# A graph-attention, scan and feed-forward kernel: the passes of its two layers alternate, the comparisons that rank its keys are spread over three passes, and its preparations are cut into smaller steps

## The chip, the core and the metric

The kernel runs on one core of a Trainium2 chip. The metric is the device time of one execution in microseconds (us). A core has five engines that run at once and wait for each other: PE (matmuls; weight loads are shown apart as PEld), DVE (vector work), ACT (activations and copies), POOL (more vector work) and SP, which here only issues DMAs. PE writes into PSUM, which has few tiles to go round; the other engines empty them.

## What is computed

The input is 16 rows of 32 channels by 512 numbers, and coordinates of 512 points for each row. Three parts follow each other, each added to the running result:

```python
x = x + xattn(ctx_4096, layernorm(x), ...)   # graph part, two layers
x = x + attn(layernorm(x), ...)              # scan part: projections, a short convolution, a masked product
x = x + ffn(layernorm(x), ...)               # feed-forward with a low-rank term
```

The graph part sorts the 512 points of every row in four ways (two Morton keys, two Hilbert keys). A point's neighbours are the ten points round it in such an order. For every point, the differences to its neighbours go through a small attention of ten by ten, a linear map and a convolution; an instance norm over the row, a leaky ReLU and the greatest over the ten neighbours give the layer's output. Layer 2 does the same with layer 1's output as its features, and a last small convolution joins the input and both layers.

```python
g1 = graph_features(f0, inds, perm1, W1, b1); h1 = lrelu(inorm(conv1(g1))); feats1 = h1.max(-1)
g2 = graph_features(feats1, inds, perm2, W2, b2); h2 = lrelu(inorm(conv2(g2))); feats2 = h2.max(-1)
out = lrelu(inorm(conv3(concat(feats, feats1, feats2))))
```

## The kernel before, in words

The change touches the graph part alone. It treats the 16 rows as four groups `g` of four rows, 128 partitions each, and makes eight **passes**, one for each group and layer. `order` (line 984) lists them: groups 0 and 1 in layer 1, then 0 and 1 in layer 2, then 2 and 3 in layer 1, then 2 and 3 in layer 2. In the code `layer` is 0 for the first layer and 1 for the second; the text calls their passes **first-layer** and **second-layer** passes, and counts passes 0 to 7. The first layer has 32 output channels, the second 64, so a matmul of `mapped` (line 874) has 128 columns in the one and 256 in the other.

A pass has 43 **blocks** (`gi`, 12 points each), and the loop of line 1019 goes through all 344 blocks as a software pipeline: one turn works on several blocks, each at another step (the number is how many blocks the step lags behind).

- `scores` (0): a mask matmul (line 805, the first matmul of a block) and 16 score matmuls (line 812) into PSUM tile `s`. `greatest` (0): DVE takes the greatest of each row (line 821). `expo` (1): PE subtracts it (line 829), ACT takes the exponential (line 834). `sums` (1) and `shares` (1): DVE sums (841) and inverts (847), POOL multiplies into `EN` (849). `turn` (3): DVE transposes it (855).
- `mapped` (0): 48 matmuls of the differences `DD` with the weights (874), which ACT copies out of PSUM (879). `outputs` (3): 32 matmuls into `h` (902). `reduce` (4) and `rest` (5): DVE takes greatest and moments out of `h` (919 to 928).
- `differences` runs six blocks ahead (`LEAD`) on POOL (line 770), out of the sorted features `fs` and the centres `crep`; SP then copies them into `DX` by DMA (line 780).

Three other kinds of work are cut into small steps (Python generators) and put between those, and every engine takes its instructions in the order in which they are issued:

- **Comparisons** (`compare`, line 535): the rank of a point is found by comparing all keys with all: a matmul of 512 columns (538) into one of two PSUM tiles `misc`, and a Sign on ACT that sums its row (539). There are 256 of them, 16 for each row. `rank_step` does one. 64 are done before the blocks begin; then each block does one (line 1033), and a second one while fewer than 128 are done (line 1042).
- **The preparation** of the next pass (`prep`, line 621): for the first layer the layernorm that gives its features `U` (lines 88 to 93); four transposes on PE (`pf`, line 634) and a copy on ACT; a split into three bf16 parts on DVE (641, 643); two casts `c16`, `c32` (647, 650) and a matmul `ph` (655). Then, for each of four rows and four chunks of points, four **one-hots** on DVE (line 723, from the ranks) and 12 matmuls with them (`place`, 689) that sort the features. The sorted row leaves PSUM by an ACT copy `so` (696), goes out to DRAM (`store`, 700), and comes back spread over partitions as `fs` (`spread`, 709); `tick` counts the steps between those. The last instruction, a DVE copy that widens `fs` (line 741), needs the last `spread` to have landed. `steps` (line 998) gives a preparation one or two of its steps a block: two while more steps are left (of a guess, `PREP` = 45) than blocks. What is left is issued all at once at block 37 (line 1047), where `differences` begins to need the next pass's `fs`.
- **The tail** of a pass (`end`, line 944): instance norm, leaky ReLU, and for the second layer the last convolution and its layernorm (`finish`, 970). A tail begins at block 3 of the next pass and takes the steps of `steps` for itself until it is done; the preparation waits for it.

The two steps that the prediction speaks of most are these (lines 646 to 657; a step ends at a `yield`):

```python
        c32 = wk.tile([P, D], F32, tag="c32", name=f"c32{key}", bufs=1)
        nc.vector.tensor_copy(c32, c16)
        yield
        hc = wk.tile([P, npair, D], F32, tag="hc", name=f"hc{key}")
        for pr in range(npair):
            ph = ps_1.tile([P, D], F32, tag="misc", bufs=2, name=f"ph{key}_{pr}")
            nc.tensor.matmul(ph, lhsT=WC[:, pr], rhs=c32, start=True, stop=True)
```

The scan and the feed-forward parts follow (from line 1055 on) and are the same in both kernels.

Of the kernel before, what the change touches and what calls it, by code (L numbers as in the profile page):

```python
# [18 lines left out]
P = 128  # L19
# [26 lines left out]
NHT = 16  # L46
LR = 18
LEAD = 6
PREP = 45


@with_exitstack
def kernel(ctx: ExitStack, tc: tile.TileContext, I, out):
# [31 lines left out]
    def layernorm_steps(pool, dst, src, key):  # L85

        st = pool.tile([P, 6], F32, tag="ln_st", name=f"lnst_{key}")
        nc.vector.bn_stats(st, src)
        mv = pool.tile([P, 2], F32, tag="ln_mv", name=f"lnmv_{key}")
        nc.vector.bn_aggr(mv, st)  # L90
        r = pool.tile([P, 1], F32, tag="ln_r", name=f"lnr_{key}")
        yield from rstd_steps(pool, r, mv[:, 1:2], 1, key)
        nc.vector.tensor_scalar(dst, src, mv[:, 0:1], r, ALU.subtract, ALU.mult)
# [282 lines left out]
def graph_part(nc, tc, cx, I, dram, id32, ones, xt, F0, layernorm_steps, rstd_steps, scan_input):  # L376
# [241 lines left out]
    def later_tile(n):  # L618
        return ps_1.tile([P, D], F32, tag="misc", bufs=2, name=f"kd{n}")

    def prep(g, layer, early=False):


# [22 lines left out]
        c16 = wk.tile([P, D], F16, tag="c16", name=f"c16{key}", bufs=1)  # L646
        nc.vector.tensor_copy(c16, src)
        yield
        c32 = wk.tile([P, D], F32, tag="c32", name=f"c32{key}", bufs=1)
        nc.vector.tensor_copy(c32, c16)  # L650
        yield
        hc = wk.tile([P, npair, D], F32, tag="hc", name=f"hc{key}")
        for pr in range(npair):
            ph = ps_1.tile([P, D], F32, tag="misc", bufs=2, name=f"ph{key}_{pr}")
            nc.tensor.matmul(ph, lhsT=WC[:, pr], rhs=c32, start=True, stop=True)
            nc.scalar.activation(hc[:, pr], ph, AF.Identity, bias=HB)
# [26 lines left out]
        pend = []  # L683

        def place():
            b, c, ohs, pp = pend.pop()
            for m, oh in ohs:
                for k in range(3):
                    nc.tensor.matmul(  # L689
                        pp[32 * m:32 * m + 32, :], lhsT=F3[k][:, c, 32 * b:32 * b + 32], rhs=oh,  # L690
                        start=(c == 0 and k == 0), stop=(c == 3 and k == 2),
                    )
            if c < 3:
                return
            so = wk.tile([P, D], F32, tag="so", name=f"so{key}_{b}", bufs=2)
            nc.scalar.copy(so, pp)
            dS = dram.tile([P, D], F32, name=f"dS{key}_{b}")

            def store():
                nc.sync.dma_start(out=dS, in_=so)  # L700

                if not early:
                    centre(b)
                later.append([3, spread])

            def spread():
                for m in range(M):
                    r = 32 * b + 8 * m
                    nc.sync.dma_start(
                        out=fs[r:r + 8, :, :D], in_=dS[32 * m:32 * m + 32].rearrange("(h c) n -> c h n", h=4)  # L710
                    )

            later.append([2, store])

        for b in range(4):
            while ranked[0] < ranks_of(4 * g + b):
                yield False
            pp = None
            for c in range(4):
                ohs = []  # L720
                for m in range(M):
                    oh = wk.tile([P, D], BF16, tag="oh", name=f"oh{key}_{b}_{m}_{c}", bufs=8)
                    nc.vector.tensor_scalar(  # L723
                        oh, it2, rank[:, c, m, 4 * g + b:4 * g + b + 1], None, ALU.is_equal
                    )
                    ohs.append((m, oh))
                    if m == 1:
                        tick()
                        yield
                if pend:  # L730
                    place()
                if c == 0:
                    pp = ps_1.tile([P, D], F32, tag="pp", name=f"pp{key}_{b}")
# [7 lines left out]
        nc.vector.tensor_copy(fs[:, :, D:], fs[:, :, D - 1:D].to_broadcast([P, 4, 4]))  # L741
        made[key] = (fs, crep, hc)

    def differences(at, gi):

# [224 lines left out]
    def finish(g, F2):  # L970
        p3 = ps_1.tile([P, D], F32, tag="misc", bufs=2, name=f"p3_{g}")
        for j, f in enumerate((F0[:, g], F1[g], *F2)):
            nc.tensor.matmul(p3, lhsT=W3[:, j], rhs=f, start=(j == 0), stop=(j == 3))
        h3 = wk.tile([P, D], F32, tag="h3", name=f"h3_{g}", bufs=1)
        nc.scalar.copy(h3, p3)
        yield
        n3 = wk.tile([P, D], F32, tag="n3", name=f"n3_{g}", bufs=1)
        yield from layernorm_steps(sm, n3, h3, f"f{g}")
        yield
        nc.vector.scalar_tensor_tensor(n3, n3, 0.2, n3, ALU.mult, ALU.max)  # L980
        nc.vector.tensor_tensor(xt[:, g], xt[:, g], n3, ALU.add)
# [5 lines left out]
    next(first)  # L987
    for _ in first:
        if ranked[0] < FIRST:
            rank_step(early_tile)  # L990
# [4 lines left out]
    for gi in range(LEAD):  # L995
        differences(0, gi)

    def steps(at, gi):


        if tails:
            if next(tails[0], tails) is tails:
                tails.pop(0)
            return
        if at + 1 >= len(order):
            return
        if at + 1 not in ahead:
            if at > 0 and gi < 4:
                return
            ahead[at + 1] = [prep(*order[at + 1]), PREP]  # L1010
        a = ahead[at + 1]
        for _ in range(2 if a[1] > NGRP - LEAD - 1 - gi else 1):
            if next(a[0], None) is False:
                break
            a[1] -= 1

    ahead = {}
    blocks = [(at, gi) for at in range(len(order)) for gi in range(NGRP)]
    for it in range(len(blocks) + 5):
# [6 lines left out]
        if gi == 0 and it < len(blocks):  # L1026
            begin(at)
        do(expo, 1)
        do(turn, 3)
# [404 lines left out]
```

## Time and profile before

| | |
|---|---|
| median of 3 runs | 2420.97 us (2415.48 to 2423.53) |
| the profiled execution's own time | 2416.21 us |
| its span, first to last instruction | 2414.5 us |
| start, to the first block | 93 us |
| the eight passes | 93 to 1358 us |
| scan and feed-forward | 1358 us to the end |
| PE, DVE, ACT, POOL busy over the span | 91%, 70%, 46%, 34% |
| mean granted TensorE clock | 0.971 |

Times in the trace count from the span's start. A row of a group of instructions gives its busy time, the mean of one, and the idle time of its engine just before them with what ended it; "issue" there means that the engine waited for nothing that the profile shows. A row of the table of windows gives, for a stretch of time, the busy time of each engine with the number of its instructions, and then PEclk, the share of its full clock that TensorE was granted. In the timeline a row is start, duration, engine, line, operation, what it writes and reads, and in brackets the idle time before it and who ended that.

### The profile page before, as it was taken

The page shows a single profiled execution, that of the slowest core. Times are in us where ns is not written, and L with a number is a line of the kernel's source. Part 1 is how long each engine was busy: PE and PEld are TensorE (multiplying, and loading weights), DVE is VectorE, ACT ScalarE, POOL GpSimd, SP SyncE. Part 2 cuts the span into 40 slices and gives each one's busy share as a digit, 9 for nine tenths or more (in the row PEclk, how much of TensorE's full clock was granted, in tenths as well). Part 3 has the DMA queues.
Part 4 walks back from the last instruction along what each step waited for, and adds up shares of the span by engine and source line. Part 5 has one row for each costly group of instructions (what it writes and reads, how often), then busy time and mean ns, then how long its engine had stood idle before and what let it go on. Part 6 is the DMA issues. An engine that isn't in the chain of part 4 may idle for free. (4 is left out here: it accounts for less than half of the span.)

```text
span 2414.5 us, 88867 instructions
## 1 busy us (share of the span) xinstructions
PE 2190.0 (91%) x39234; PEld 1248.1 (52%) x39234; DVE 1699.6 (70%) x3674; ACT 1100.1 (46%) x2023; POOL 831.6 (34%) x897
## 2 busy tenths in 40 slices
PE   5699798999999778789999789999999999999979
PEld 2255455667676454567777544444444444444422
DVE  8487797888899888889999866554553625446643
ACT  6677566667665334345555322333332424333331
POOL 2165556445446565664655300020210202021200
PEclk9799899999999999999999899999999999999989
DMA  1323232132132231422211212213112121210000
GB/s 48 80 55 77 48 80 57 43 73 47 36 70 56 54 77 46 91 52 65 63 34 41 91 53 77 75 32 91 53 53 71 35 91 46 73 55 20 27 36 18
DMA packets 121625, 137.99 MB, mean 57 GB/s; under 512 B 18398, under 2 KB 79506, under 8 KB 121154
## 3 DMA queue, kind: packets, MB, share of 16 engines
q1 hardware_dynamic: 121240, 132.32, 21.9%
q8 instruction: 308, 5.05, 0.9%
q14 instruction: 77, 0.63, 0.1%
HBM read 77.02 MB, written 12.85 MB: 37 GB/s over the span
## 5 line engine op out<-in xcount | busy, mean ns | idle before, releaser
L849 POOL TENSOR_TENSOR EN<-e,rz 128x480 f32<-128x480 f32 x344 | 342.4, 995 | 554.4 <-DVE rz L847 430.1
L874 PE MATMUL u<-WA,DD 128*32 128x128 bf16 (+1 forms) x16512 | 418.6, 250 | 26.4 <-issue 26.4
L874 PEld LDWEIGHTS <-DD 128*32 128x32 f16 x16512 | 338.8, 98 | 72.7 <-issue 68.5
L879 ACT COPY us<-u 128x512 f32<-128x512 f32 x516 | 302.0, 587 | 149.5 <-PE u L874 131.8
L834 ACT ACTIVATE e<-s,smc 128x480 f32<-128x480 f32 x344 | 227.6, 662 | 290.7 <-PE s L829 248.0
L770 POOL TENSOR_TENSOR DD<-fs,crep 128x480 f16<-128x480 f32 (+2 forms) x344 | 349.6, 1017 | 0.0
L902 PEld LDWEIGHTS h<-e,us 128*32 128x32 f32 (+1 forms) x11008 | 248.8, 126 | 144.1 <-issue 65.6
L902 PE MATMUL h<-e,us 128*32 128x30 f32 (+1 forms) x11008 | 282.0, 211 | 37.1 <-DVE e L855 19.4
L821 DVE TENSOR_REDUCE c<-s 128x16 bf16<-128x480 f32 x344 | 220.7, 642 | 107.0 <-PE s L812 104.4
L1132 DVE SCALAR_TENSOR_TENSOR cyh<-ppch,t_conv_w,cyh 128x496 f32<-128x496 f32 (+2 forms) x192 | 137.4, 716 | 221.7 <-ACT cyh L1127 217.7
L1208 POOL TENSOR_TENSOR da<-lei,dA 128x512 f32<-128x512 f32 x32 | 40.6, 1269 | 611.8 <-PE pl L1213 577.5
L1281 PE MATMUL po<-wo,gs 128*128 128x512 f32 x512 | 240.5, 605 | 10.4 <-DVE xt L1284 10.3
L1120 PE MATMUL ppch<-hT,winch 128*128 128x512 f32 x512 | 232.2, 593 | 0.0
L1120 PE MATMUL ppg<-hT,wing 128*128 128x512 f32 x512 | 231.9, 593 | 0.0
L855 DVE STREAM_TRANSPOSE e<-EN 128x512 f32<-128x512 f32 x344 | 224.4, 652 | 0.0
L841 DVE TENSOR_REDUCE z<-e 128x16 f32<-128x480 f32 x344 | 219.5, 638 | 0.0
L539 ACT ACTIVATE sgn<-kd 128x512 bf16<-128x512 f32 x256 | 153.0, 598 | 56.2 <-PE kd L538 52.4
L812 PEld LDWEIGHTS <-DD 128*32 128x32 f16 x5504 | 81.7, 96 | 163.2 <-issue 129.5
L723 DVE TENSOR_SCALAR oh<-it,rank 128x512 bf16<-128x512 f16 x512 | 158.0, 368 | 7.5 <-PE pp L689 7.5
L812 PE MATMUL s<-DX,DD 128*32 128x120 f16 x5504 | 143.1, 223 | 19.6 <-DMA DX<-DD 16.2
L1120 PEld LDWEIGHTS ppch<-hT,winch 128*128 128x128 f32 x512 | 93.7, 190 | 122.7 <-issue 122.3
L1120 PEld LDWEIGHTS ppg<-hT,wing 128*128 128x128 f32 x512 | 95.8, 190 | 114.0 <-issue 114.0
(327 smaller groups left out, 2845.6 us busy)
## 6 DMA issues: line engine op xcount, KB each, us to landing
DX<-DD SPq DMA_DIRECT2D x456, 90.0 KB
wo<-in_out_proj SPq DMA_DIRECT2D x64, 256.0 KB
wing<-in_in_proj SPq DMA_DIRECT2D x64, 256.0 KB
winch<-in_in_proj SPq DMA_DIRECT2D x64, 256.0 KB
crep<-dC SPq DMA_DIRECT2D x128, 64.0 KB
dS<-so SPq DMA_DIRECT2D x32, 256.0 KB
fs<-dS SPq DMA_DIRECT2D x128, 64.0 KB
wincB<-in_in_proj SPq DMA_DIRECT2D x8, 256.0 KB
```

The lines of the kernel that those rows point to most:

```text
L770: nc.gpsimd.tensor_tensor(d[:, :, m0 - n0:n1 - n0], win, crep[:, :, m0:n1].unsqueeze(3).to_broadcast([P, 4, n1 - m0, K]), ALU.subtract,)
L812: nc.tensor.matmul(s[rh, j * 4 * QB:(j + 1) * 4 * QB].rearrange("p (b q) -> p b q", b=4), lhsT=d[:, h, c0:c0 + 32], rhs=dx[:, h, :, c0:c0 ...
L821: nc.vector.tensor_reduce(c, live["s", at, gi].rearrange("p (i q) -> p i q", q=QB), AX.X, ALU.max, negate=True)
L834: nc.scalar.activation(e, s.rearrange("p (i q) -> p i q", q=QB), AF.Exp, scale=smc)
L841: nc.vector.tensor_reduce(z, e, AX.X, ALU.add)
L849: nc.gpsimd.tensor_tensor(en[:, :, :QB], e, rz.unsqueeze(2).to_broadcast([P, NI, QB]), ALU.mult)
L855: nc.vector.transpose(e.rearrange("p i q -> p (i q)"), en.rearrange("p i q -> p (i q)"))
L874: nc.tensor.matmul(u[rh, jj], lhsT=d[:, h, c0:c0 + 32], rhs=WA[k][:, h].rearrange("p b o -> p (b o)"), start=(jj == 0 and k == 0), stop=(k ...
L879: nc.scalar.copy(us[:, j - jj:j + 1], u)
L902: nc.tensor.matmul(h[r:r + co, pr, q0:q0 + QB], lhsT=us[:, j, b * co:(b + 1) * co], rhs=e[:, 4 * j + b, :QB], start=npair > 1, stop=True, ...
L1120: nc.tensor.matmul(pp, lhsT=w[:, k], rhs=hT[:, k], start=(k == 0), stop=(k == 3))
L1281: nc.tensor.matmul(po, lhsT=gs[:, i, q * P:(q + 1) * P], rhs=wo[i], start=(i == 0), stop=(i == TG - 1))
```

## The change

The constants and the order of the passes change; `wanted` says how many comparisons should be done by the end of each pass, and the loop stops at that; steps are cut finer by added `yield`s; one-hots come in tiles of two. The code also gets a branch that would keep one-hots of the first layer in DRAM and load them for the second; it is for the groups in `KEPT`, which is empty, so that nothing of it is issued and `at_hand` is always false.

```diff
-PREP = 45
+PREP = (49, 46, 42)
+SPARE = 3
...
         nc.vector.bn_stats(st, src)
+        yield
         mv = pool.tile([P, 2], F32, tag="ln_mv", name=f"lnmv_{key}")
...
+    KEPT = ()
...
             yield from layernorm_steps(sm, src, xt[:, g], f"g{g}")
+            yield
         dC = dram.tile([P, D], F32, name=f"dC{key}")
...
+        def share():
...
+            c32 = wk.tile([P, D], F32, tag="c32", name=f"c32{key}", bufs=1)
+            nc.vector.tensor_copy(c32, c16)
+            yield
+            yield
+            hc = wk.tile([P, npair, D], F32, tag="hc", name=f"hc{key}")
+            for pr in range(npair):
+                ph = ps_1.tile([P, D], F32, tag="misc", bufs=2, name=f"ph{key}_{pr}")
+                nc.tensor.matmul(ph, lhsT=WC[:, pr], rhs=c32, start=True, stop=True)
+                nc.scalar.activation(hc[:, pr], ph, AF.Identity, bias=HB)
+                yield
+            made[key][2] = hc
+
+        made[key] = [None, None, None]
+        if not at_hand:
+            yield from share()
...
+                ohs = [
+                    wk.tile([P, 2, D], BF16, tag="oh", name=f"oh{key}_{b}_{c}_{i}", bufs=4) for i in range(2)
+                ]
...
-        place()
+        while pend:
+            place()
+            tick()
+            yield
...
         nc.vector.scalar_tensor_tensor(n3, n3, 0.2, n3, ALU.mult, ALU.max)
+        yield
         nc.vector.tensor_tensor(xt[:, g], xt[:, g], n3, ALU.add)
...
-    order = [(0, 0), (1, 0), (0, 1), (1, 1), (2, 0), (3, 0), (2, 1), (3, 1)]
+    order = [(0, 0), (1, 0), (0, 1), (2, 0), (1, 1), (3, 0), (2, 1), (3, 1)]
...
-            ahead[at + 1] = [prep(*order[at + 1]), PREP]
+            g, layer = order[at + 1]
+            ahead[at + 1] = [prep(g, layer), PREP[layer + at_hand(at + 1)]]
         a = ahead[at + 1]
-        for _ in range(2 if a[1] > NGRP - LEAD - 1 - gi else 1):
+        for _ in range(2 if a[1] > NGRP - LEAD - SPARE - gi else 1):
...
+    def wanted(at):
+
+        return ranks_of(4 * min(NBG, 1 + sum(layer == 0 for _, layer in order[:at + 1])) - 1)
...
-        rank_step(later_tile)
+        if ranked[0] < wanted(at):
+            rank_step(later_tile)
...
-        if ranked[0] < 8 * 4 * M:
+        if ranked[0] < wanted(at) and (at == 0 or gi % 2):
             rank_step(later_tile)
         do(outputs, 3)
+        if at == 0 and gi < 8:
+            rank_step(later_tile)
```

The built programs hold the same instructions; only their order differs:

| pass | layer before / after | comparisons before / after | layer that is prepared there, before / after | block of the copy of line 741, before / after |
|---|---|---|---|---|
| 0 | first / first | 75 / 64 | first / first | 37 / 34 |
| 1 | first / first | 43 / 64 | second / second | 36 / 34 |
| 2 | second / second | 43 / 0 | second / first | 36 / 33 |
| 3 | second / first | 31 / 64 | first / second | 36 / 37 |
| 4 | first / second | 0 / 0 | first / first | 36 / 33 |
| 5 | first / first | 0 / 0 | second / second | 36 / 37 |
| 6 | second / second | 0 / 0 | second / second | 36 / 34 |
| 7 | second / second | 0 / 0 | none | none |

More of the change, by code (lines that the diff above doesn't have):

```diff
@@ L619, in later_tile @@
         return ps_1.tile([P, D], F32, tag="misc", bufs=2, name=f"kd{n}")
+    KEPT = ()
+    kept = {}
+    transfers = []
     def prep(g, layer, early=False):
@@ L644, in prep @@
                 yield
[L646 to L656, printed above, removed]
-            yield
+        at_hand = layer == 1 and g in KEPT
+        def share():
+            c16 = wk.tile([P, D], F16, tag="c16", name=f"c16{key}", bufs=1)
+            nc.vector.tensor_copy(c16, src)
+            yield
+            c32 = wk.tile([P, D], F32, tag="c32", name=f"c32{key}", bufs=1)
[12 more added lines that the diff above has]
+            yield from share()
         crep = big.tile([P, 4, D], F32, tag="crep", name=f"crep{key}", bufs=2)
@@ L685, in place @@
         def place():
-            b, c, ohs, pp = pend.pop()
-            for m, oh in ohs:
+            b, c, ohs, pp = pend.pop(0)
+            for m in range(M):
                 for k in range(3):
                     nc.tensor.matmul(
-                        pp[32 * m:32 * m + 32, :], lhsT=F3[k][:, c, 32 * b:32 * b + 32], rhs=oh,
+                        pp[32 * m:32 * m + 32, :], lhsT=F3[k][:, c, 32 * b:32 * b + 32], rhs=ohs[m // 2][:, m % 2],
                         start=(c == 0 and k == 0), stop=(c == 3 and k == 2),
@@ L719, in prep, with keep_it @@
             for c in range(4):
[L720 to L727, printed above, removed]
+                if c == 0:
+                    pp = ps_1.tile([P, D], F32, tag="pp", name=f"pp{key}_{b}")
+                if at_hand and len(pend) == 2:
+                    place()
[4 more added lines that the diff above has]
+                ]
+                for i, oh in enumerate(ohs):
+                    if at_hand:
+                        transfers.append((oh, kept[g, b, c, i]))
+                        continue
+                    for j in range(2):
+                        m = 2 * i + j
+                        nc.vector.tensor_scalar(
+                            oh[:, j], it2, rank[:, c, m, 4 * g + b:4 * g + b + 1], None, ALU.is_equal
+                        )
+                    if layer == 0 and g in KEPT:
+                        kept[g, b, c, i] = dram.tile([P, 2, D], BF16, name=f"k{key}_{b}_{c}_{i}")
+                        def keep_it(to=kept[g, b, c, i], oh=oh):
+                            nc.scalar.dma_start(out=to, in_=oh)
+                        later.append([1, keep_it])
+                    if i == 0:
                         tick()
                         yield
-                if pend:
+                if pend and not at_hand:
                     place()
-                if c == 0:
-                    pp = ps_1.tile([P, D], F32, tag="pp", name=f"pp{key}_{b}")
                 pend.append((b, c, ohs, pp))
@@ L736, in prep @@
                 yield
-        place()
+        while pend:
+            place()
+            tick()
+            yield
+        if at_hand:
+            for _ in share():
+                tick()
+                yield
         while later:
@@ L741, in prep @@
         nc.vector.tensor_copy(fs[:, :, D:], fs[:, :, D - 1:D].to_broadcast([P, 4, 4]))
-        made[key] = (fs, crep, hc)
+        made[key][:2] = fs, crep
     def differences(at, gi):
@@ L980, in finish @@
         nc.vector.scalar_tensor_tensor(n3, n3, 0.2, n3, ALU.mult, ALU.max)
+        yield
         nc.vector.tensor_tensor(xt[:, g], xt[:, g], n3, ALU.add)
     made = {}
-    order = [(0, 0), (1, 0), (0, 1), (1, 1), (2, 0), (3, 0), (2, 1), (3, 1)]
+    order = [(0, 0), (1, 0), (0, 1), (2, 0), (1, 1), (3, 0), (2, 1), (3, 1)]
     keys = [f"{layers[layer][0]}_{g}" for g, layer in order]
     first = prep(*order[0], early=True)
-    next(first)
+    for _ in range(4):
+        next(first)
     for _ in first:
@@ L996, in graph_part, with at_hand @@
         differences(0, gi)
+    def at_hand(at):
+        g, layer = order[at]
+        return layer == 1 and g in KEPT
     def steps(at, gi):
@@ L1003, in steps @@
                 tails.pop(0)
-            return
+            if at + 1 >= len(order) or not at_hand(at + 1):
+                return
         if at + 1 >= len(order):
@@ L1007, in steps @@
         if at + 1 not in ahead:
-            if at > 0 and gi < 4:
+            if at > 0 and gi < 4 and not at_hand(at + 1):
                 return
-            ahead[at + 1] = [prep(*order[at + 1]), PREP]
+            g, layer = order[at + 1]
+            ahead[at + 1] = [prep(g, layer), PREP[layer + at_hand(at + 1)]]
         a = ahead[at + 1]
-        for _ in range(2 if a[1] > NGRP - LEAD - 1 - gi else 1):
+        for _ in range(2 if a[1] > NGRP - LEAD - SPARE - gi else 1):
             if next(a[0], None) is False:
@@ L1028, in graph_part @@
         do(expo, 1)
+        for oh, of in transfers:
+            nc.scalar.dma_start(out=oh, in_=of)
+        transfers.clear()
         do(turn, 3)
```

## The prediction

> **What bounds the kernel now.** First the table of windows, one row for each pass (cut where the first matmul of a pass, line 805, starts):
>
> ```profile
> core 0: us, PE busy (x) PEld busy (x) DVE busy (x) ACT busy (x) POOL busy (x), PEclk, DMA share, GB/s
> 93.00:264.00 171.00, 137.53 (x4414) 76.68 (x4412) 117.23 (x267) 112.33 (x247) 91.44 (x108) 0.90 0.30 63
> 264.00:408.00 144.00, 127.77 (x4480) 75.08 (x4481) 121.85 (x274) 87.99 (x182) 86.04 (x96) 0.99 0.31 67
> 408.00:583.00 175.00, 172.10 (x4465) 120.01 (x4467) 143.76 (x333) 113.45 (x226) 87.38 (x97) 0.98 0.25 55
> 583.00:755.00 172.00, 168.62 (x4452) 120.45 (x4451) 152.74 (x367) 105.81 (x207) 85.85 (x96) 0.99 0.25 55
> 755.00:907.00 152.00, 119.82 (x4431) 76.67 (x4434) 132.00 (x308) 58.82 (x101) 85.75 (x95) 0.93 0.28 61
> 907.00:1049.00 142.00, 113.23 (x4470) 72.03 (x4468) 123.10 (x276) 58.43 (x96) 87.01 (x97) 0.98 0.30 66
> 1049.00:1205.00 156.00, 152.84 (x4424) 116.15 (x4427) 141.16 (x332) 83.76 (x139) 86.45 (x96) 0.98 0.26 60
> 1205.00:1358.00 153.00, 145.32 (x4251) 113.59 (x4245) 143.69 (x337) 83.06 (x155) 79.93 (x81) 0.99 0.17 37
> ```
>
> Second-layer passes (2, 3, 6, 7) are bound by PE: it idles 3 of 175 us in pass 2. First-layer passes (0, 1, 4, 5) are not: it idles 16 to 34 us in each. By the timeline the passes take 170.9, 143.9, 174.6, 172.1, 152.7, 141.2, 156.0 and 148.7 us (to the last block's start).
>
> Then ends of passes with no one-hots in them, about eleven blocks of passes 1 and 5, nine of 2 and 6:
>
> ```profile
> 370.00:405.00 35.00, 30.01 (x1114) 17.87 (x1115) 24.82 (x50) 21.53 (x45) 22.29 (x31) 1.00 0.25 59
> 1012.00:1045.00 33.00, 25.64 (x1096) 16.59 (x1094) 25.52 (x52) 14.32 (x23) 23.19 (x32) 1.00 0.31 67
> 546.00:579.00 33.00, 33.00 (x896) 23.92 (x893) 27.19 (x57) 22.70 (x45) 18.92 (x28) 1.00 0.22 46
> 1172.00:1201.00 29.00, 29.00 (x893) 23.14 (x891) 26.58 (x56) 16.53 (x27) 18.89 (x28) 1.00 0.25 55
> ```
>
> Rows one and three hold a comparison in every block, two and four none. In a second-layer pass a comparison costs its PE time: pass 2 less pass 6, 18.6 us over 43, is **0.43 us**. In a first-layer pass eleven of them add 4.4 us of PE work and, by exact block starts, 1.34 us of time (34.56 less 33.22): **0.12 us** each. The rest fills gaps of this kind, in the middle of one group of matmuls:
>
> ```profile
> 1022.06 0.26 PE L902 MATMUL h<-e,us 128*32 128x30 f32 x6 [1.76 <-issue]
> ```
>
> PE waits there for nothing that the profile shows; waits of "issue" come every few blocks in first-layer passes, whose blocks hold as many PE instructions as second-layer ones in less time. The page has 308 packets of instructions (5.05 MB) for 88867 instructions, so I read these gaps as the supply of instructions. [...]
>
> Third, PE's longest waits. One in pass 6, and the clock after it:
>
> ```profile
> 1077.26 1.48 PE L874 MATMUL u<-WA,DD 128*32 128x256 bf16 x48
> 1081.90 2.08 PE L655 MATMUL ph<-c,WC 128*128 128x512 f32 x2 [3.16 <-DVE c L650]
> 1083.91 1.92 PE L902 MATMUL h<-e,us 128*64 128x30 f32 x32
> ```
> ```profile
> 1082.00:1087.00 5.00, 5.00 (x52) 2.65 (x56) 1.43 (x4) 1.25 (x2) 1.98 (x2) 0.50 0.33 74
> ```
>
> PE comes to `ph` in the block in which DVE is only given its cast (`c32`), waits 3.16 us, and then runs at half clock: the six groups from `ph` on take 8.01 us where their like one block later take 4.87. The wait costs 3.16 + 3.1 = **6.3 us**. The same wait stands in passes 1 (3.26), 2 (2.29) and 5 (3.27). The transposes `pf` wait for the layernorm likewise, 3.38 us in pass 3, 2.38 in pass 0, and in pass 4:
>
> ```profile
> 803.07 1.11 PE L634 MATMUL pf<-id,U 128*128 128x128 f32 x4 [5.40 <-DVE U L93]
> ```
>
> Last the end of pass 0, DVE and SP:
>
> ```profile
> 249.29 0.17 DVE L741 COPY fs<-fs 128x16 f32<-128x16 f32 x1 [13.59 <-DMA fs<-dS]
> ```
> ```profile
> 239.61 0.34 SPq L700 DMA_DIRECT2D dS<-so  x1
> 240.00 1.38 SPq L665 DMA_DIRECT2D crep<-dC  x4
> 241.92 1.30 SPq L709 DMA_DIRECT2D fs<-dS  x4
> ```
>
> The preparation ended late, the rest was issued at once, and DVE, with all reductions queued behind line 741, stood until `fs` landed. PE idled 10.56 us. Blocks 38 and 39 took 18.7 us instead of 2 x 3.04 (the mean of such blocks in pass 5): 12.6 us lost.
>
> **The change, part by part,** as a sum over passes; a pass of the changed kernel is set beside the pass of before that is most like it.
>
> *Second-layer passes.* Passes 2, 4, 6 and 7 hold no comparison now, so pass 6 of before is their pattern. By the built order `ph` is now issued at least a block after its cast: -6.3. Pass 6: 149.7. Passes 2 and 4 prepare a first-layer pass: one `ph` fewer (-1.1, from its 1.12), but a layernorm. Its statistics stand a block earlier now; yet the last step and `pf` still fall into one block (8). DVE then has two reductions (1.2 us), four small operations (0.19 each) and `U` (0.55), 2.5 us, against some 1.1 us of `mapped` on PE after the scores: 1.4 us of wait, more if DVE is behind. No row has this order; the bounds are 0 and the 5.40 of pass 4. Of those 5.40, 1.5 were statistics and ACT, and 1.8 the tail's two operations just before (1.11, 0.69), so I take 2.1, nearest to that row. The half clock after it I take as 1.2 us, between 0 and 3.1. That a wait of 2.29 us was followed by half clock is seen in pass 2 (PEclk 0.50 in 447 to 453 us). [...] So 156.0 - 6.3 - 1.1 + 3.3 = 151.9 each. Pass 7 stays at 148.7; its finer steps move small DVE work (between -2 and +2; I take 0, PE is 98% busy there). Sum 602.2 against 174.6 + 172.1 + 156.0 + 148.7 = 651.4: **-49.2**.
>
> *First-layer passes.* A comparison costs between 0.12 us (at one a block) and 0.43. At 1.5 a block the gaps (33 - 25.6 = 7.4 us in eleven blocks) are mostly filled, and blocks with one-hots carry PE's 12 `place` matmuls too; I take 0.20, nearer the row of the same layer.
> - Pass 0: the copy of line 741 comes two blocks after the last `place` and no key loads stand before its store. From `so` to a landed `fs` it took 10.4 us in pass 3 and 12.1 in pass 4; DVE needs about 5 for two blocks (7.4 for three in pass 4), so it waits 5 to 7, of which PE sees some two thirds (4.68 on DVE were 2.86 on PE): 4.5 in place of 12.6, -8.1. Half of the `pf` wait goes, -1. Three comparisons a block in the first eight make ACT the fullest engine there (3 x 0.79 + 0.59 + 0.66 = 3.6 us a block): +2, bounds 0 and 4. 11 comparisons fewer, -1.3. 162.5.
> - Pass 1: `ph` wait, half of 3.26 since DVE was full there anyway, with some half clock: -2. Late `fs`, -1.4. 21 more comparisons, +4.2. 144.7.
> - Passes 3 and 5 follow a second-layer pass, as pass 4 did, whose long tail they carry on DVE; so 152.7 is the pattern. No layernorm: -6 (5.40 and some half clock). One more `ph`, +1.1. The finer steps and the long tail make their preparations start at block 15, and 46 steps at two a block last until block 37: the name says three blocks ahead, the built order has line 741 at 37, right behind the last `spread`. By the reckoning of pass 0 PE loses 4.5 and 5.5 (in pass 5 SP has a `DX` copy before the `spread`, as in pass 4), in place of 2.9. Pass 3 has 64 comparisons, +12.8. Pass 3: 162.2. Pass 5: 150.4.
>
> Sum 619.8 against 170.9 + 143.9 + 152.7 + 141.2 = 608.7: **+11.1**.
>
> *At nothing:* tiles of two one-hots (as many DVE instructions and bytes; the two chunks in flight stay), the branch for `KEPT`, the start (ACT, POOL and SP have the same order there) and everything behind the passes. Key loads still come eight blocks or more before their comparison; if one were late, PE would stand for the rest of a DMA, some 5 us by the `spread`.
>
> Sum: -49.2 + 11.1 = -38.1. 2416.2 - 38.1 = **2378 us**. The profiled execution's time lies 4.8 under the median of the three runs and within their spread of 8, so I leave it so.
>
> **Rivals.**
> - *A: comparisons cost their PE time everywhere.* (85 x 0.23 - 11 x 0.31) = +16: 2394. For it: at 1.5 a block a first-layer block has little slack. Against it: rows one and two above.
> - *B: the late ends of passes 3 and 5 cost as much as pass 0's did,* 12.6 each instead of 4.5 and 5.5: +15: 2393. For it: they end at block 37 as that one did. Against it: they are a block further, and no key loads hold up SP.
> - *C: the waits vanish.* `pf` finds its `U` (-6.6), `fs` costs what it did in pass 4 (-6), comparisons 0.12 (-6): 2359. For it: DVE has slack where nothing is prepared.
> - *D: slower.* A comparison borrows one of the two `misc` tiles, and in a first-layer pass PE waits for the Sign before it. At a full Sign on ACT (598 + 195 ns) instead of 0.20 us, the 128 of passes 1 and 3 cost 76 more: 2454. It turns the sign from 0.50 us each on. For it: three a block in pass 0, ACT behind. Against it: before, pass 0 did two a block, and PE waited for line 539 at line 538 for 1.4 us in all.
> - That the change does not do what it says is B in part: the spare blocks are there in passes 0, 1, 2, 4 and 6 only.
>
> **How the numbers follow.** Forecast 0.49, A 0.18, B 0.10, C 0.15, D 0.08. About 0.3%, 7 us, can be told from no change. Of D, 0.03 falls within that and 0.05 beyond; the others are faster: 0.92, 0.03, 0.05. The forecast's own terms reach from 2365 to 2392 (the `pf` waits from 0 to 6 each, comparisons 0.12 to 0.30, ACT 0 to 4); with A, B and C and their overlaps 2350 to 2403. That leaves out D, and the ends where A and B or all of C's terms fall together.
>
> **What would show it.** Passes 2 and 4 near 152 us with blocks of 3.2 and, with one-hots, 3.9; pass 3 near 162 with PE over 90% busy, and waits of "issue" fewer than in pass 5; no wait of PE for `c32`; short ones for `U` in block 8 of passes 2 and 4; line 741 waiting 4 to 8 us at block 37 of passes 3 and 5. Wrong it would be if pass 3 took 175, if PE waited for line 539, or if the second-layer passes did not come down.

## The result, and the profile after

| | before | changed |
|---|---|---|
| median, in the same job | 2418.22 us (2412.85 to 2423.53, 4 runs) | 2378.44 us (2376.64 to 2383.11, 4 runs) |
| profiled execution: own time, span | 2416.21, 2414.5 | 2376.64, 2374.9 |
| mean granted TensorE clock | 0.971 | 0.978 |

The ratio is 0.9836, with a 95% interval of [0.9813, 0.9858]: faster by 1.6%. The forecast was 2378. That the two agree so closely is luck: the passes show that the number came out of larger errors that cancel:

| pass | before | predicted | after | after less predicted | PE idle, before / after |
|---|---|---|---|---|---|
| 0 | 170.9 | 162.5 | 163.7 | +1.2 | 33.5 / 32.9 |
| 1 | 143.9 | 144.7 | 141.9 | -2.8 | 16.2 / 10.4 |
| 2 | 174.6 | 151.9 | 154.9 | +3.0 | 2.9 / 3.9 |
| 3 | 172.1 | 162.2 | 151.4 | **-10.8** | 3.4 / 12.8 |
| 4 | 152.7 | 151.9 | 156.7 | +4.8 | 32.2 / 6.3 |
| 5 | 141.2 | 150.4 | 149.3 | -1.1 | 28.8 / 32.8 |
| 6 | 156.0 | 149.7 | 154.7 | **+5.0** | 3.2 / 3.3 |
| 7 | 148.7 | 148.7 | 144.6 | -4.1 | 7.7 / 5.2 |
| sum | 1260.1 | 1222.0 | 1217.2 | -4.8 | |

The passes lose 42.9 us; the first block starts 0.6 later, and from the last block to the end of the span it takes 2.8 longer (1064.0 instead of 1061.2). Together that is the span's 39.6.

The table of windows of the changed kernel, one row for each pass:

```profile
core 0: us, PE busy (x) PEld busy (x) DVE busy (x) ACT busy (x) POOL busy (x), PEclk, DMA share, GB/s
94.00:258.00 164.00, 131.05 (x4413) 75.47 (x4416) 116.97 (x268) 104.06 (x226) 92.13 (x109) 0.93 0.31 66
258.00:400.00 142.00, 131.62 (x4516) 76.17 (x4512) 121.39 (x275) 100.38 (x224) 84.96 (x95) 1.00 0.33 68
400.00:554.00 154.00, 150.13 (x4411) 114.73 (x4397) 143.63 (x341) 82.79 (x139) 86.64 (x96) 0.99 0.28 60
554.00:706.00 152.00, 139.22 (x4520) 80.09 (x4517) 130.43 (x300) 100.77 (x229) 85.94 (x96) 0.97 0.28 62
706.00:862.00 156.00, 149.72 (x4411) 114.44 (x4412) 143.21 (x341) 83.10 (x139) 86.74 (x96) 1.00 0.28 61
862.00:1012.00 150.00, 117.19 (x4456) 75.11 (x4457) 131.29 (x301) 59.35 (x101) 87.50 (x97) 0.98 0.28 61
1012.00:1166.00 154.00, 150.66 (x4415) 115.39 (x4414) 141.14 (x332) 83.51 (x138) 85.26 (x95) 0.99 0.28 60
1166.00:1311.00 145.00, 139.78 (x4132) 109.27 (x4128) 138.29 (x329) 80.84 (x151) 79.33 (x81) 1.00 0.18 39
```

Rows four and six are the ones to read together. Both are first-layer passes that follow a second-layer pass and prepare one. Row four holds 64 comparisons, 22 us more of PE's time (139.22 against 117.19), and is 2.1 us longer; PE's waits of "issue" come to 2.3 us in it, in 5 places, against 15.3 us in 18 in row six. Rows three, five, seven and eight are the second-layer passes, with no comparison: PE is still over 95% busy in each.

The waits have changed places. What PE waited for ahead of `ph` (us in total, times), before and after:

```profile
  DVE c L650: 23.8, 8
```
```profile
  DVE c L660: 2.5, 2
```

Of the 2.5 us left, 2.2 are in the start and 0.3 in pass 0: the wait for the cast `c32` is gone from the passes. In its place stands one that the kernel before had mainly in pass 0. All waits of DVE at its copy that widens `fs` (line 780 now, 741 before):

```profile
L780 DVE COPY fs<-fs x8: 174/174/175, 102.0 to 1139.6; 128x16 f32<-128x16 f32 x8
...
  DMA fs<-dS: 35.5, 7
```

It waits in all seven passes that prepare another: 7.56, 2.15, 0.30, 8.17, 4.70, 8.84 and 3.82 us in passes 0 to 6 (before: 13.59, 2.96, 0.99, 1.56, 4.68, 1.10, 0.00). The longest but one, in pass 3, on DVE and on SP's queue:

```profile
682.89 0.25 DVE L886 RECIPROCAL rz<-z 128x16 f32<-128x16 f32 x1
691.31 0.17 DVE L780 COPY fs<-fs 128x16 f32<-128x16 f32 x1 [8.17 <-DMA fs<-dS]
691.39 0.70 DVE L894 STREAM_TRANSPOSE e<-EN 128x512 f32<-128x512 f32 x1
```
```profile
681.88 0.54 SPq L716 DMA_DIRECT2D dS<-so  x1
682.46 1.41 SPq L681 DMA_DIRECT2D crep<-dC  x4
685.79 1.32 SPq L725 DMA_DIRECT2D fs<-dS  x4
```

The sorted row goes out at 681.88, its copies back are issued from 685.79, and they have landed at 691.31; for all that time the transpose of line 894 stands behind a copy of 0.17 us, and PE, which needs `e`, stands for 5.99 us. PE's gaps of this kind are 6.32, 5.99, 2.56, 7.73 and 2.07 us in passes 0, 3, 4, 5 and 6: 24.7 together.

The waits for `U` ahead of `pf`, in pass 2 and then in pass 4:

```profile
430.01 0.66 PE L641 MATMUL pf<-id,U 128*128 128x128 f32 x4 [2.43 <-DVE U L95]
430.60 1.30 PE L941 MATMUL h<-e,us 128*64 128x30 f32 x32
```
```profile
735.76 0.66 PE L641 MATMUL pf<-id,U 128*128 128x128 f32 x4 [2.33 <-DVE U L95]
736.34 1.12 PE L941 MATMUL h<-e,us 128*64 128x30 f32 x32
```

Both are as foretold in place and length (2.1 was the estimate). After the first the same 32 matmuls take 1.30 us instead of 1.12, after the second they don't.

### The profile page after: what moved, and what is told of

The parts are those of the page before. It is cut to its first block, busy times and chain, and to the rows that moved or that the text cites. A ratio compares the mean times of both kernels' runs of the same rounds, so it can differ in the third digit from the quotient of the medians.

```text
span 2374.9 us, 88834 instructions
## 1 busy us (share of the span) xinstructions
PE 2172.0 (91%) x39234; PEld 1243.6 (52%) x39234; DVE 1694.5 (71%) x3674; ACT 1093.6 (46%) x2023; POOL 831.4 (35%) x897
## 5 line engine op out<-in xcount | busy, mean ns | idle before, releaser
L913 PE MATMUL u<-WA,DD 128*32 128x128 bf16 (+1 forms) x16512 | 412.5, 248 | 19.4 <-issue 19.1
L1189 DVE SCALAR_TENSOR_TENSOR cyh<-ppch,t_conv_w,cyh 128x496 f32<-128x496 f32 (+2 forms) x192 | 137.5, 716 | 221.9 <-ACT cyh L1184 217.9
L1338 PE MATMUL po<-wo,gs 128*128 128x512 f32 x512 | 240.5, 605 | 10.4 <-DVE xt L1341 10.3
```

Source lines behind the costliest of these rows:

```text
L913: nc.tensor.matmul(u[rh, jj], lhsT=d[:, h, c0:c0 + 32], rhs=WA[k][:, h].rearrange("p b o -> p (b o)"), start=(jj == 0 and k == 0), stop=(k ...
L1338: nc.tensor.matmul(po, lhsT=gs[:, i, q * P:(q + 1) * P], rhs=wo[i], start=(i == 0), stop=(i == TG - 1))
```

## The experiments

Each one's median stands beside that of the kernel before in the same job, 2415.82 to 2419.02 us. Lengths of single passes come from one profiled execution. Unchanged passes show how far they scatter: pass 5 of the kernel before takes 141.2, and 145.5 in e2, where nothing in it is changed; and pass 1 of the changed kernel takes 141.9, and 137.9 in both e4 and e9, which leave it as it is.

### e1: the comparisons back where they were

```diff
-        if ranked[0] < wanted(at):
-            rank_step(later_tile)
+        rank_step(later_tile)
...
-        if ranked[0] < wanted(at) and (at == 0 or gi % 2):
+        if ranked[0] < 8 * 4 * M:
             rank_step(later_tile)
         do(outputs, 3)
-        if at == 0 and gi < 8:
-            rank_step(later_tile)
```

> The changed kernel, but with the comparisons as the kernel before spreads them: one a block until all are done, a second while fewer than 128 are done. So 75, 43, 43, 31 of them fall into passes 0, 1, 2, 3 instead of 64, 64, 0, 64; pass 2 is a second-layer pass. My theory (a comparison costs 0.43 us in a second-layer pass, and next to nothing, 0.03 to 0.20, in a first-layer one): pass 2 from 154.9 to 173, passes 1 and 3 down by 1 to 10 in all; the kernel at 2386 to 2396, some 0.987 to 0.991 of before. Rival A (0.43 everywhere): the total stays at 2378. Rival E (the gain comes from the finer steps, not from the comparisons): the total stays too, and pass 2 does not grow by more than 5.

2388.99 us (2387.61 to 2390.16), ratio 0.9874 [0.9854, 0.9894]: 10.5 of the 39.8 us are lost. The passes: 163.2, 136.7, 169.4, 148.2, 160.0, 150.2, 155.0, 144.7. Pass 2, with 43 comparisons again:

```profile
394.80:564.20 169.40, 167.85 (x4459) 118.51 (x4457) 145.59 (x342) 112.91 (x226) 87.35 (x97) 1.00 0.27 56
```

It is 14.5 longer, 0.34 us for each; rivals A and E, by which the total would have stayed, fall. Passes 1 and 3 lose 21 and 33 comparisons and 8.4 us together, 0.16 each. Pass 0 is as long as in the changed kernel, though its late copy is worse again (DVE waits 12.51, PE 11.26, with the last `store` at block 38 instead of 33 and eight loads of keys ahead of it on SP). What pays for that is the first sixteen blocks: 66.4 us instead of 72.1, of which 0.9 is block 0. So three comparisons a block in the first eight cost some 4.8 us.

### e2: the new spread of the comparisons alone, in the kernel before

Passes 0, 1 and 4 are the first-layer passes that get 64 each in that order.

```diff
-        rank_step(later_tile)
+        if ranked[0] < wanted(at):
+            rank_step(later_tile)
...
-        if ranked[0] < 8 * 4 * M:
+        if ranked[0] < wanted(at) and (at in (0, 4) or gi % 2):
             rank_step(later_tile)
         do(outputs, 3)
+        if at in (0, 4) and gi < 8:
+            rank_step(later_tile)
```

> The kernel before with the new spread of the comparisons alone (its old order of passes, old steps, old ends): 64 each in the first-layer passes 0, 1 and 4, three a block in the first eight blocks of passes 0 and 4. My theory: passes 2 and 3 lose 18.5 and 13.3, pass 4 gains 2 to 13, pass 0 loses some 8 because its preparation ends earlier; the kernel at 2380 to 2395, 0.984 to 0.990 of before, so that this part alone is most of the gain. Rival A: 2410 to 2420. Rival E: 2405 or more.

2395.62 us (2390.96 to 2399.15), ratio 0.9906 [0.9879, 0.9933]: -22.4, just above the theory's range. The passes: 159.2, 148.2, 155.0, 164.7, 157.2, 145.5, 154.8, 148.7. Pass 2 loses 19.6 and pass 3 7.4, which is 0.46 and 0.24 for each comparison; pass 4 gains 64 comparisons and 4.5 us, 0.07 each. Pass 1 becomes 4.3 longer: its copy of line 741 waits 6.96 instead of 2.96 us. The largest surprise is pass 0, -11.7. A preparation can't make the one-hots of a row before that row is ranked. With three comparisons a block in the first eight, the one-hots in pass 0 begin at block 5 instead of 8, and the last `store` goes out at block 33 instead of 38. SP's queue from there:

```profile
224.09 0.34 SPq L700 DMA_DIRECT2D dS<-so  x1
224.47 1.39 SPq L665 DMA_DIRECT2D crep<-dC  x4
225.96 3.09 SPq L780 DMA_DIRECT2D DX<-DD  x4
229.09 1.83 SPq L709 DMA_DIRECT2D fs<-dS  x4
```

The copy of line 741, still at block 37, waits 0.00 instead of 13.59 us, and the last nine blocks take 27.3 instead of 40.8. Eight loads of keys that stood ahead of the last `store` in the kernel before (at 235.77 to 239.52) are gone from there too, but they can have held it up by 3.9 us at most; the rest is the preparation's earlier end. So about half of what the spread of the comparisons gains in this kernel comes from the end of pass 0.

### e3: the preparation's steps coarse again

```diff
-PREP = (49, 46, 42)
+PREP = (46, 45, 42)
...
-            yield from layernorm_steps(sm, src, xt[:, g], f"g{g}")
-            yield
+            norm = layernorm_steps(sm, src, xt[:, g], f"g{g}")
+            next(norm)
+            yield from norm
...
             nc.vector.tensor_copy(c32, c16)
             yield
-            yield
```

> The changed kernel, with the steps of a preparation cut as before (statistics with their inverse root, the layernorm's last step with the transposes pf, the cast c32 with ph at the next step), and the guesses 46 and 45. My theory: PE waits again 2 to 3.3 us for c32 in passes 1, 3, 5, 6, and 3 to 5 us for U in passes 2 and 4, with half clock after; pass 6 plus 6, passes 1, 3, 5 plus 2 each, 2 and 4 plus 2 each: plus 10 to 19, 2388 to 2397. Rival E would have plus 25 or more; rival F (a wait taken away only comes back at the next wait of the same block): 0 to plus 4.

2391.49 us (2389.1 to 2394.66), ratio 0.9885 [0.9864, 0.9907]: +13.0 against the changed kernel. What PE waits for ahead of `ph` here:

```profile
  DVE c L661: 22.8, 7
```

The waits for `c32` are back, 3.08, 3.09, 3.83 and 3.17 us in passes 1, 3, 5 and 6, and those for `U` are 3.54 and 3.17 in passes 2 and 4. Every pass but 0 and 7 becomes 1.7 to 4.5 us longer, pass 6 by 4.2. The finer steps are worth 13 us, and both readings at the ends, that they are worth nothing or most of the gain, fall.

### e4: comparisons that nobody reads, one kind of pass against the other

The kernel is the changed one with work added: two comparisons a block in pass 5 (first layer) and one a block in pass 6 (second layer).

```diff
+        if at in (5, 6):
+            extra(2 * it)
...
+        if at == 5:
+            extra(2 * it + 1)
```

> The changed kernel with comparisons added whose result nobody reads: two in every block of pass 5 (first layer, 86) and one in every block of pass 6 (second layer, 43). My theory: pass 5 from 149.3 to 152 to 166 (0.03 to 0.20 each), pass 6 from 154.7 to 173 (0.43 each). Rival A: pass 5 to 186. Rival D (PE waits for the Sign on ACT): pass 5 to 186 or more, with PE idle for the Sign.

2391.17 us, one run. Passes 5 and 6 of the changed kernel, then of this one:

```profile
862.00:1011.30 149.30, 116.51 (x4449) 74.94 (x4447) 130.83 (x300) 59.26 (x100) 86.80 (x97) 0.98 0.28 61
1011.30:1166.00 154.70, 151.34 (x4417) 115.56 (x4416) 141.60 (x332) 83.60 (x138) 85.96 (x96) 0.99 0.27 60
```
```profile
859.90:1011.80 151.90, 144.75 (x4530) 79.95 (x4528) 129.87 (x300) 112.61 (x271) 85.74 (x96) 0.98 0.29 61
1011.80:1181.20 169.40, 168.58 (x4461) 118.64 (x4459) 143.24 (x334) 113.35 (x226) 87.28 (x97) 1.00 0.26 56
```

In pass 5, 28 us more of PE's work make the pass 2.6 us longer: 0.03 us for each of 86. The waits of "issue" that PE has in it in the changed kernel (15.3 us in 18) are all gone. In pass 6, 43 make it 14.7 longer: 0.34 each. Rival A (their PE time everywhere) and rival D (the Sign on ACT) would have had pass 5 over 30 us longer; both fall.

### e5: one spare block instead of three

```diff
-SPARE = 3
+SPARE = 1
```

> The changed kernel with the spare blocks back at one (the guesses 49 and 46 kept): the copy that widens fs is issued at blocks 35, 36, 35, 37, 35, 37, 36 instead of 34, 34, 33, 37, 33, 37, 34. What the trace of the changed kernel shows: with two steps a block to the end, the copy follows the last store by three blocks, too soon for its DMAs, and DVE waits 7.6, 2.2, 4.7 and 3.8 us for it in passes 0, 1, 4 and 6. Theory G (the three spare blocks cost time, since the copy is issued before its data can be there): minus 6 to minus 14, 2364 to 2372, with passes 4 and 6 down by 2 to 4 each. Rival: the spare blocks gain, as they were meant to, and this is 3 to 10 slower; or no difference within 4.

2373.2 us (2366.26 to 2377.28), ratio 0.9816 [0.9789, 0.9842], which overlaps that of the changed kernel. The passes: 157.2, 146.2, 158.3, 154.5, 152.3, 151.6, 151.8, 144.6. Passes 0, 4 and 6 lose 6.5, 4.4 and 2.9 us; passes 1, 2, 3 and 5 gain 4.3, 3.4, 3.1 and 2.3, with the copy now waiting 7.17 us at block 37 of pass 1 and 4.87 at block 36 of pass 2. The median is 5.2 us lower, between theory G and "no difference". The three spare blocks gain nothing that can be measured: they move the wait for `fs` from some passes into others.

### e6: the order of the passes as before

```diff
-    order = [(0, 0), (1, 0), (0, 1), (2, 0), (1, 1), (3, 0), (2, 1), (3, 1)]
+    order = [(0, 0), (1, 0), (0, 1), (1, 1), (2, 0), (3, 0), (2, 1), (3, 1)]
...
-        if ranked[0] < wanted(at) and (at == 0 or gi % 2):
+        if ranked[0] < wanted(at) and (at in (0, 4) or gi % 2):
             rank_step(later_tile)
         do(outputs, 3)
-        if at == 0 and gi < 8:
+        if at in (0, 4) and gi < 8:
```

> The changed kernel with the passes in the order of before. The comparisons then fall, 64 each, into passes 0, 1 and 4, all of the first layer, three a block in the first eight blocks of passes 0 and 4. So this undoes the alternation alone. My theory (what counts is that no comparison is in a second-layer pass, not the alternation): within 8 of the changed kernel, 2370 to 2386; only one first-layer pass, 4, carries a long tail, which may gain some 5, but pass 3 prepares a first-layer pass late, which may cost as much. Rival: the alternation itself carries the gain, 2395 or more.

2374.56 us, the median of three executions (2373.92 to 2382.64; a fourth took 5220.57 us and is left out), ratio 0.9835 [0.9804, 0.9865]: the changed kernel's. Its passes: 163.1, 140.3, 152.1, 168.3, 154.7, 137.5, 155.0, 144.6. Pass 3, a second-layer pass behind another, is long (PE waits 2.90 us for `U` in its block 16 and 5.19 for `e` in its block 38), and pass 5 is as much shorter. No gain of the alternation itself can be measured.

### e7: the copy that widens `fs` issued five blocks later

It is moved out of the preparation into `differences`, to block 42, so that DVE never stands at it; POOL, whose work it precedes, still waits for `fs`.

```diff
-        nc.vector.tensor_copy(fs[:, :, D:], fs[:, :, D - 1:D].to_broadcast([P, 4, 4]))
         made[key][:2] = fs, crep
...
         fs, crep, _ = made[keys[at]]
+        if gi == 5:
+            nc.vector.tensor_copy(fs[:, :, D:], fs[:, :, D - 1:D].to_broadcast([P, 4, 4]))
```

> The changed kernel with the copy that widens fs issued five blocks later than differences begins to read it (it is needed only by a pass's last block), so that DVE does not stand for the DMAs of fs. My theory (the waits of DVE on that copy, 7.6, 2.2, 0.3, 8.2, 4.7, 8.8, 3.8 us in passes 0 to 6, stop the pipeline, with half clock after them): pass 0 minus 6 to 8, passes 4 and 6 minus 3 to 4 each, pass 1 minus 1, passes 3 and 5 minus 3 to 4 each (there POOL itself needs fs at that time): minus 15 to 24, 2354 to 2364. Rival H (the wait only passes to POOL): minus 0 to minus 5.

2359.74 us (2356.97 to 2365.77), ratio 0.9772 [0.9748, 0.9796]: 18.7 us faster than the changed kernel. What DVE still waits for at the copy:

```profile
  DMA kr<-others: 9.3, 1
  issue: 0.9, 2
```

No wait for `fs` is left there (the 9.3 us are at the first pass, as before). The passes: 157.8, 139.1, 154.4, 147.9, 154.1, 146.9, 151.9, 144.8, which is 5.9, 2.8, 0.5, 3.5, 2.6, 2.4 and 2.8 us less in passes 0 to 6. In passes 3 and 5 PE still stands for 3.79 and 4.42 us, now at block 40, where POOL's differences come late because `fs` does.

### e8: three steps a block where a preparation is far behind

On top of e7:

```diff
-        for _ in range(2 if a[1] > NGRP - LEAD - SPARE - gi else 1):
+        left = NGRP - LEAD - SPARE - gi
+        for _ in range(3 if a[1] > 2 * left else 2 if a[1] > left else 1):
```

> As the kernel with the late copy, and a preparation takes three steps a block while it is more than twice behind, so that those of passes 3 and 5 end two blocks sooner. My theory: another 3 to 10 less, 2348 to 2360, from passes 3 and 5. Rival: six one-hots a block hold up DVE's reductions, and what is won at the end is lost there: within 3 of the kernel with the late copy.

2357.62 us (2354.36 to 2362.04), ratio 0.9755 [0.973, 0.9781], not to be told from e7. The waits at block 40 of passes 3 and 5 are gone, but PE now waits for one-hots (1.49 and 2.36 us at block 19), and the passes are 148.5 and 146.6 instead of 147.9 and 146.9. The wait was exchanged for another.

### e9: many very small instructions on PE

The kernel is the changed one with 32 matmuls of 8 columns, and so 32 weight loads, added to each block of passes 5 and 6; nobody reads their result.

```diff
+            nc.tensor.matmul(
+                t[r:r + 32, c:c + 8], lhsT=idb[:, r:r + 32], rhs=idb[:, 0:8], start=(j < 4), stop=True,
+                skip_group_check=True,
+            )
...
+        if at in (5, 6):
+            tiny(it)
```

> The changed kernel with 32 small matmuls (8 columns) and their weight loads added in every block of passes 5 and 6, into a PSUM tile that nobody reads: 64 PE instructions a block beside the 200 or so that a block has, some 0.4 us of PE time (the 32 matmuls of outputs, of 30 columns, take 0.46). Two comparisons a block, 4 instructions and 0.8 us of PE time, made pass 5 only 2.6 us longer. Theory S (a first-layer pass goes at the pace at which PE gets its instructions, some 14 ns each): pass 5 plus 30 to 45, from 149.3 to 179 to 194. Rival T (it is PE's latency chain with DVE that sets the pace, and PE time up to its idle 32 us is free): pass 5 plus 0 to 6. In pass 6, which PE time bounds: plus 14 to 25 by both.

2429.36 us, one run. Passes 5 and 6:

```profile
859.50:1043.30 183.80, 132.27 (x5820) 87.93 (x5818) 129.22 (x301) 59.28 (x100) 86.86 (x97) 0.95 0.23 51
1043.30:1221.50 178.20, 167.90 (x5794) 129.09 (x5792) 143.84 (x333) 83.54 (x139) 86.53 (x96) 0.99 0.25 54
```

Beside the rows of the changed kernel under e4, pass 5 has 16 us more of PE's work, less than the 28 that the large comparisons of e4 brought, and is 34.4 us longer instead of 2.6. PE's idle time rises from 32.8 to 51.5, and the waits of "issue" in it from 15.3 to 45.6. Pass 6 becomes 23.5 longer for 16.6 of work. Both lengths are theory S's, and rival T falls. The work didn't fill the gaps; it made more of them. One, inside the added group itself:

```profile
931.85 0.33 PE L556 MATMUL kd<-idb 128*32 128x8 bf16 x26
934.03 0.21 PE L556 MATMUL kd<-idb 128*32 128x8 bf16 x6 [1.86 <-issue]
```

What the gaps follow is the number of PE's instructions (the two counts of a row added): 183.80 us over 11638 are 15.8 ns each, 178.20 over 11586 in pass 6 are 15.4, and pass 1 of e7, 139.1 us over the same 9028 as in the changed kernel, comes to 15.4 too. The 14 ns of theory S were the author's estimate.

### e10: one more block between `U` and `pf`

On top of e7:

```diff
-PREP = (49, 46, 42)
+PREP = (50, 46, 42)
...
             yield from layernorm_steps(sm, src, xt[:, g], f"g{g}")
             yield
+            yield
...
-    for _ in range(4):
+    for _ in range(5):
         next(first)
```

> This is e7_widen_late with the preparation's norm cut once more: the multiplication by V that writes U comes one block earlier than the matmul and copy that read U into pf (five steps of the first rows' norm instead of four, so that as many come ahead of the first pass). Theory: the 2.43 and 2.33 us that TensorE waits for U in passes 2 and 4 of the changed kernel, and the slower clock after the first of them, are the price of U and pf in one block. With a block between them passes 2 and 4 of e7 (154.4 and 154.1) lose 2 to 4 us each, and the time goes from 2359.7 to 2351 to 2357. Rival: the wait only moves to the next thing that DVE has late (the copy of the widened rows in block 42, or the one-hots of the blocks with an added step), passes 2 and 4 stay within 1 us of 154, and the time stays within 3 us of 2359.7.

2356.64 us (2349.16 to 2363.82), ratio 0.9752 [0.9726, 0.9779]. What PE waits for ahead of `pf`, in e7 and in e10:

```profile
  DVE U L95: 15.0, 6
```
```profile
  DVE U L95: 3.3, 1
```

The waits in the passes are gone (the 3.3 us are in the start). Passes 2 and 4 take 152.8 and 151.9, 1.6 and 2.2 us less than in e7, at the theory's lower end; pass 3 takes 2.7 more and pass 6 1.1 more, so that the total can't be told from e7's. The mechanism holds; that it gains time overall is not shown. e7, e8 and e10 all beat both kernels, the kernel before by 2.3 to 2.5%, and can't be ranked among themselves.

## Why the prediction was right, and where it wasn't

**The sign and the place were right.** The gain comes from second-layer passes, which PE fills, and the first-layer passes took the comparisons in. The sum by halves: second-layer passes -40.5 instead of -49.2 (610.9 against 651.4), first-layer passes -2.4 instead of +11.1 (606.3 against 608.7). The errors of 8.7 and 13.5 us have opposite signs.

**The comparison in a second-layer pass (0.43 us)** was about right in size, if rather high: 0.34 in e1 and in e4, 0.46 and 0.24 in passes 2 and 3 of e2.

**The comparison in a first-layer pass (0.20, bounds 0.12 to 0.43) is the mis-sized term**, and its lower bound was too high: the 0.12 rested on 1.34 us between two single stretches, which is less than a pass scatters. Pass 3 against pass 5 gives 2.1 / 64 = 0.03 us, e4 0.03, pass 4 of e2 0.07, passes 1 and 3 of e1 0.16; all 268 of them together cost 17.6 us, 0.07 each. Pass 3 was forecast 12.8 us for its 64 and came out 10.8 below. The reason given, that waits of "issue" are gaps which a matmul can fill, held: in e4 the comparisons made them vanish. e9 says why the price is nearer to nothing than the row of 0.12: a comparison is one matmul of 512 columns and one load, two instructions in a block of some 207. In a pass whose pace is set by the number of instructions, 128 more of them should cost 128 x 15.4 ns = 2.0 us, which is what pass 3 showed, and the 172 of e4's pass 5 should cost 2.6, as they did; the 8.4 us of e1's 54 are more than this explains, and stay open beside the scatter of about 4 us a pass. e9's 34.4 us for work of 16 speak for instructions that come too slowly there, and so do the places of the waits of "issue" over 0.4 us: 256 PE instructions apart, or a multiple of that, and each 1.22 to 1.75 us behind a packet of 16384 bytes on the instruction queue, as the last section shows.

**The late `fs`** was foreseen at the right place in passes 3 and 5 (block 37, PE 4.5 and 5.5; measured 5.99 and 7.73, waits of DVE 8.17 and 8.84) and in pass 0 (4.5; measured 6.32). In the kernel before, the wait of pass 0 was so long mainly because the last `store` came at block 38, not 33 (e2); the loads of keys account for 3.9 of the 13.59 us at most. But the step failed in passes 4 and 6. I had taken the three spare blocks for a cover there; in fact the pace of two steps a block, kept up to the end, brings the copy so close behind the last `store` that SP's copies of `DX` between `store` and `spread` make it late (in pass 4 the `store` goes out at 818.74, the copies of `DX` take SP 3.11 us from 825.51 on, and the `spread` follows at 828.66; in pass 6 it is 1124.78, 2.53 us from 1131.79 on, and 1134.37): 4.70 and 3.82 us on DVE, 2.56 and 2.07 on PE. With one spare block (e5) DVE waits 0.00 in both. Pass 6 was to lose 6.3 with the wait for `c32`; the wait went, blocks 35 and 36 became 6.1 and 4.0 long instead of 3.2, and the pass fell by 1.3. e7, which removes this wait alone, in all passes, gets 18.7 us back. The moved wait is where much of the possible gain had gone. Rival B, 12.6 us at the ends of passes 3 and 5, fell.

**The waits for `c32` and `U`** behaved as said. `c32`: gone, and back in e3, at 13 us for all of the finer steps. `U`: 2.43 and 2.33 for 2.1. The half clock of 1.2 us after it came in pass 2 (block 9 took 4.4 instead of 3.2) and not in pass 4 (3.2); the last section says what parts the two.

**Pass 0's first blocks** cost more than the 2 us that I gave three comparisons a block: some 4.8 by e1. **Pass 7** lost 4.1 us where I had 0, with bounds of 2. In ten kernels with the cut tail it takes 144.6 to 144.9, in the two without it (the kernel before and e2) 148.7; the order of the passes, the comparisons and the preparation's steps were each undone without bringing it back. What remains are the two `yield`s that cut the tail, in its layernorm and ahead of its last step; they were not run by themselves, so that this cause is not shown.

**The account of the gain.** The comparisons out of second-layer passes are worth 10.5 us when they are undone (e1) and 22.4 by themselves (e2). Much of the difference is the end of pass 0. Both kernels send the last `store` there at block 33; e2 has the copy at block 37, where it waits 0.00, and gains 11.7, while the changed kernel has it at block 35, where it waits 7.56, and gains 6.4 in the last nine blocks (34.4 instead of 40.8) and gives 2.3 back in the first sixteen. The finer steps are worth 13.0 (e3), the tail's cut perhaps 4 (not shown), the order (e6) and the spare blocks (e5) nothing that can be measured. Pieces taken out one by one, these make some 28 of the 39.8 us; what one frees another can fill, and no run says where the rest comes from.

## What to carry to other kernels

Ask of each stage not only how busy the engine is but what its idle time is made of: here the gaps of "issue" in pass 5 took 86 large matmuls, 28 us of work, for 2.6 us (e4), while 1376 small ones, 16 us of work, cost 34.4 (e9), and the passes of e9 took 15.4 to 15.8 ns for each PE instruction. When a wait is removed from an engine, look for the next instruction on it that depends on a DMA, however cheap: a copy of 0.17 us that waited for a round trip through DRAM held up all of DVE, and issuing it later was worth 18.7 us, nearly half of what the whole change had gained. And a total that comes out right is no proof: compare the forecast with the measurement stage by stage.

## What the hardware showed unexpectedly

- **PE's longer waits of "issue" stand 256 instructions apart, each behind a packet on the instruction queue.** In the kernel before, 41 of PE's waits of "issue" in the eight passes are over 0.4 us long. They stand a whole multiple of 256 PE instructions apart, give or take one (matmuls, loads and its semaphore instructions counted), and each ends 1.22 to 1.75 us after a packet of 16384 bytes on the instruction queue has landed; the 35 of the changed kernel do the same. How many such packets there are follows PE's instructions. This is the queue (packets, MB, share of the 16 DMA engines) before and in e9, where 22 packets more go with 5504 more matmuls and loads:

```profile
q8 instruction: 308, 5.05, 0.9%
q8 instruction: 330, 5.41, 1.0%
```

  Where two such waits stand 256 instructions apart, they come some 3.9 us apart (the median, before and in e9), or 15.2 ns for each of 256 instructions. That is near the pace of whole passes: 15.4 in pass 1 of e7 and in pass 6 of e9, 15.8 in pass 5 of e9, where PE idles 51.5 us all the same. So I read these waits, as the prediction did, as waits for the supply of instructions; a limit on PE's own rate alone would give no reason for these places.
- **The granted clock fell to half where PE had idled for some 2 us within one stretch of 3.41 us.** The 32 matmuls after a wait of 2.43 us took 1.30 us, those after one of 2.33 took 1.12, as they did at 835.11, while 2.29 us in the kernel before was followed by half clock (PEclk 0.50 in 447 to 453 us). The granted clock of the three microseconds behind the waits of pass 2 and pass 4:

```profile
430.00:433.00 3.00, 2.99 (x50) 1.98 (x54) 1.71 (x4) 0.80 (x2) 1.98 (x2) 0.73 0.23 87
736.00:739.00 3.00, 3.00 (x86) 2.38 (x88) 1.89 (x4) 1.25 (x2) 1.98 (x2) 1.00 0.65 180
```

  In each of the twelve traces the granted clock changes only at whole multiples of 3.41 us from its other changes. Over the passes of all twelve, PE idled for over 2.0 us in 75 such stretches of 3.41 us that ran at full clock, and 74 of them were followed by half clock (15 of 15 in the traces of the two kernels); of those with under 1.4 us none was, and in between it went both ways (4 of 21 in the two kernels). The wait of 2.43 us has 2.05 us in one stretch and the one of 2.29 us has 2.14; the one of 2.33 us lies across two, with 1.73 and 0.60. So the two waits of pass 2 reach 2 us of idle time in one stretch and that of pass 4 does not.
